# Moving the first attention scores ahead of four running-maximum steps, and adding unit-matrix products at the start of a one-core block kernel

## The chip, the core and the metric

The kernel runs on one core of a Trainium2 chip. The metric is the device time of one execution in microseconds (us); several executions are timed and the median is given. A separate execution was recorded by the hardware profiler; times inside it are counted from the start of its span.

## What is computed

The input is x of 8 sequences, 512 tokens, 128 features (float32). With xn = layernorm(x), the output is x + attention(xn) + ffn(xn). Cut to what matters:

```
q, k: (b, s, 8 heads, 2, 8)      v: (b, s, 8 heads, 16)
scores = einsum('bqhif,bkhif->ibhqk', q, k) * 8 ** -0.5
att    = softmax(scores)[0] - diff_weight * softmax(scores)[1]
o      = einsum('bhqk,bkhe->bqhe', att, v)
attention = (rms_normalized(o) * norm_w) @ Wo.T + bo, times (1 - diff_weight)
gates  = sigmoid(xn @ Wg); the best 2 of 8 experts per token, weights normalized
ffn    = (shared expert + weighted sum of 2 routed experts) / 3
```

Each expert is silu(x @ W1) * (x @ W3) @ W2 with 256 inner features. The matrices are float32 throughout.

## The kernel before, in words

**Tiling.** A sequence b has NT = 4 token tiles of 128. Its 8 heads are worked in four pairs w; a pair has u = 0, 1. In the tensors qst and kst (two of each, taken in turn by the sequences) head 2w+u is one slab of 128 partitions by 512 tokens; the two halves of the partitions (ROWS) are the two halves i of the differential attention.

**Two passes over the scores.** The softmax needs the maximum over keys per query before the exponential. So `maxima(b, w)` (L786) goes through eight steps for a pair (u by t): two matmuls into the PSUM tile mx (L795) and one reduction on VectorE into the tile most (L802). The tile mx has one buffer; for the first pair alone (b = w = 0) every second step uses the buffer of sc instead. After the eighth step the maxima are split into two parts (L808, L809) and `shift(b, w)` (L825) puts them into spare rows of qst, so that the scores come out with the maximum already subtracted. For the first pair this goes by a TensorE transpose (L829, pm), a copy on ScalarE (L831, first_rows) and two DMAs of SP's queue (L820). `scores(b, w, c, u)` (L840) then makes two matmuls for one key tile (L844, sc) and the exponential on ScalarE (L852, pe); `weigh` multiplies by the values (L863, av). `next_maxima(n)` (L1049) takes the next n steps of all maxima in order; with 8 sequences, 4 pairs, 8 steps there are 256.

**Order of the work.** The order of instructions on every engine is the order of the program, written out by hand. It has a start-up part (L1062 to L1188) and a main loop (L1215 to L1251) of 128 steps of two half steps each. A half step makes one `scores` and one step of maxima, which runs ahead by a fixed number of steps. Beside these, `pieces(step)` (L1190) picks other work from a list of jobs with due steps, by estimated cost (ROOM) and free PSUM banks: norms and gates of later sequences, routing, the experts, the shared expert, the folding of results. A job's parts come at "soon" or "late" places of a step. In the first half step the job prepare(1) makes pq (L727), in the third pv (L771) and a transpose px (L236).

**Lead of the maxima.** AHEAD is 11: start-up makes 11 steps of maxima before the loop (eight of pair 0, three of pair 1). The loop adds one more in its first half step (`turns <= 1`, L1241), so that the lead is 12 steps from then on.

**Start-up in the order of TensorE.** Four weight transposes (L1090, pw); four transposes of xn (L236, px); head(0, 0), head(0, 1) (L1118, pd, each followed by a ScalarE step L1120 and a VectorE step L1123 that write the first slabs of qst and kst); maxima step 1; head(1, 0); step 2; head(1, 1); the products pq of the other six heads (L727); steps 3 to 8 with px of sequence 1, pv (L771), gate products (L249) between; then steps 9 to 11. `keep_clock()` (L1148) is a product of the unit matrix with xnT whose result (idle) nobody reads. It stands once before step 4, before step 6 (after the gate products), before step 7 and before step 8, and twice at each of steps 9, 10 and 11 (L1170 to L1173). In the trace one such product shows as two MATMUL records.

**Copies of sequence 0.** prepare(0) splits q and k in an upper and a lower part (L738, L740), and sixteen DMAs (`copy`, L753) spread them into rows of qst and kst. For sequence 0 those of qst are issued from SP's queue and those of kst from ScalarE's queue, four each for upper and lower.

**Other names.** L184 is the VectorE memset of heads 2 to 7 of kst[0] to 1.0. L1095 is a VectorE copy of pw, L213 to L217 are the statistics of the norm. The pool ps_3 holds three PSUM buffers of one bank (tag mm) that the temporary products take in turn; ps_1 holds single ones (av, sc, mx).

Of the kernel before, what the change touches and what calls it, by code (L numbers as in the profile page):

```python
# [11 lines left out]
F32 = mybir.dt.float32  # L12
# [19 lines left out]
def kernel(  # L32
# [52 lines left out]
    nc = tc.nc  # L85
    B, S, E = x.shape
    NT = S // P
    NE, _, FF = We1.shape
# [19 lines left out]
    def small_psum(name):  # L108
        return ps_3.tile([P, S], F32, tag="mm", name=name)
# [26 lines left out]
    ident = const.tile([P, P], F32, name="ident")  # L136
# [41 lines left out]
    kst = []  # L178
# [28 lines left out]
    def norm(b):  # L207

        xt = xn[b]
        stats = p2.tile([P, NT, 6], F32, tag="stats", name=f"stats_{b}")  # L210
        both = p2.tile([P, NT, 2], F32, tag="both", name=f"both_{b}")
        for t in range(NT):
            nc.vector.bn_stats(stats[:, t, :], xt[:, t, :])  # L213
        for t in range(NT):
            nc.vector.bn_aggr(both[:, t, :], stats[:, t, :])
        rstd = p2.tile([P, NT], F32, tag="rstd", name=f"rstd_{b}")
        nc.vector.tensor_scalar(rstd, both[:, :, 1], LN_EPS, None, ALU.add)  # L217
        nc.gpsimd.tensor_tensor(rstd, rstd, minus_half, ALU.pow)
        yield
        for t in range(NT):  # L220

            (nc.gpsimd if b else nc.vector).tensor_scalar(  # L222
                xt[:, t, :], xt[:, t, :], both[:, t, 0:1], rstd[:, t : t + 1], ALU.subtract, ALU.mult
            )
        yield
# [6 lines left out]
    def turn(b):  # L232

        px = small_psum(f"px_{b}")
        for t in range(NT):
            nc.tensor.transpose(px[:, t * P : (t + 1) * P], xn[b][:, t, :], ident)  # L236
        xnT = p3.tile([P, S], F32, tag="xnT", name=f"xnT_{b}")
        return xnT, px
# [306 lines left out]
    turns = 0  # L545
# [169 lines left out]
    def prepare(b):  # L715

        st = state[b]
        if "xnT" not in st:
            yield 0.45, 1
            st["xnT"], px = turn(b)  # L720
            yield "late"
            nc.scalar.copy(st["xnT"], px)
        xnT = st["xnT"]
        yield 1.75, 2
        pqs = [small_psum(f"pq_{b}_{i}") for i in range(2)]
        for i in range(2):
            nc.tensor.matmul(  # L727
                pqs[i],
                w_c[:, i].rearrange("p i f u -> p (i f u)") if b else w_rest[:, i],
                xnT,  # L730
                start=True,
                stop=True,
            )
        parts = []
        for i in range(2):
            yield ("soon", "late")[i]
            upper = p1.tile([P, S], F32R, tag=f"upper{i}", name=f"upper_{b}_{i}")
            nc.scalar.copy(upper, pqs[i])  # L738
            lower = p1.tile([P, S], F32R, tag=f"lower{i}", name=f"lower_{b}_{i}")
            nc.vector.tensor_tensor(lower, pqs[i], upper.bitcast(F32), ALU.subtract)  # L740
            parts.append((upper, lower))
        q, k = qst[b % 2], kst[b % 2]

        def no_shift():
            for half in range(2):
                nc.sync.dma_start(
                    out=q[64 * half + SHIFT : 64 * half + SHIFT + 2]
                    .bitcast(F32)
                    .rearrange("p u s -> p (u s)"),
                    in_=noughts,  # L750
                )

        def copy(part, i, s):  # L753

            row_of = (2 * part + s, part + 2 * s)[i]
            first = 0 if b else 2
            for half in range(2):
                (nc.scalar if b == 0 and i else nc.sync).dma_start(
                    out=(q, k)[i][64 * half + row_of : 64 * half + STACK : 4, first:, :].bitcast(F32),
                    in_=parts[i][part][64 * half : 64 * half + F * (H - first), :].bitcast(F32),  # L760
                )

        if b > 1:
            copies.append(no_shift)
        for part, i in ((0, 0), (0, 1), (1, 0), (1, 1)):
            for s in range(2):
                copies.append(lambda part=part, i=i, s=s: copy(part, i, s))
        yield 0.9, 1
        pv = small_psum(f"pv_{b}")
        for t in range(NT):  # L770
            nc.tensor.matmul(  # L771
                pv[:, t * P : (t + 1) * P],
                xnT[:, t * P : (t + 1) * P],
                w_t[:, 0, :],
                start=True,
                stop=True,
            )
        yield "late"
        nc.scalar.copy(
            vals[b % 2].rearrange("p t h e -> p (t h) e")[:, :, 0:DH],  # L780
            pv.rearrange("p (n e) -> p n e", e=DH),
        )
# [57 lines left out]
    def scores(b, w, c, u):  # L840

        sc = ps_1.tile([P, 2, S], F32, tag="sc", name=f"sc_{b}_{w}_{c}_{u}")
        for i in range(2):
            nc.tensor.matmul(  # L844
                sc[:, i, :],
                kst[b % 2][ROWS[i], 2 * w + u, c * P : (c + 1) * P],
                qst[b % 2][ROWS[i], 2 * w + u, :],
                start=True,
                stop=True,
            )  # L850
        pe = p4.tile([P, 2, S], F32, tag="pe", name=f"pe_{b}_{w}_{c}_{u}")
        nc.scalar.activation(pe, sc, AF.Exp, scale=F**-0.5)  # L852
        return pe
# [111 lines left out]


    STEPS = 4 * NT
    AHEAD = 11
    MIX = 30
    EACH = 4.65  # L970
    ROOM = 2.25
# [49 lines left out]
    def run(part):  # L1021
        for _ in part:
            pass
# [25 lines left out]
    def next_maxima(n):  # L1049
        for _ in range(n):  # L1050
            found = next(tiles, None)
            if found is None:
                return
            b, w, k = found
            if k == 0:
                streams[b, w] = maxima(b, w)
            next(streams[b, w])
            if k == 7:
                run(streams.pop((b, w)))
                shift(b, w)  # L1060

    with tc.manual_schedule():  # L1062
# [3 lines left out]

        norms = {b: norm(b) for b in range(B)}
        next(norms[0])  # L1070
        rows = const.tile([P, 5], F32, name="rows")
# [13 lines left out]
            nc.vector.tensor_scalar(signs[:, i : i + 1], lower, -2.0, 1.0, ALU.mult, ALU.add)  # L1085
        run(norms[0])

        pw = ps_1.tile([P, S], F32, tag="av", name="pw")
        for i in range(4):
            nc.tensor.transpose(pw[:, i * P : (i + 1) * P], w_raw[:, i, :], ident)  # L1090
# [13 lines left out]
        xnT, px = turn(0)  # L1104
# [37 lines left out]
            w = pw[:, i * P : (i + 1) * P]  # L1142
            nc.scalar.copy(w_c[:, i], w.rearrange("p (u i f) -> p i f u", i=2, f=F))
        nc.scalar.copy(w_t.rearrange("p i e -> p (i e)"), pw[:, 2 * P :])

        idle = ps_1.tile([P, S], F32, tag="av", name="idle")

        def keep_clock():  # L1148
            nc.tensor.matmul(idle, ident, xnT, start=True, stop=True)  # L1149

        next_maxima(1)
        state[1]["xnT"], px = turn(1)
        nc.scalar.copy(state[1]["xnT"], px)
        keep_clock()
        next_maxima(1)
        run(first)
# [6 lines left out]
        next_maxima(1)  # L1163
        gates(1, state[1]["xnT"])
        held.append(pgs[0])
        keep_clock()
        next_maxima(1)
        keep_clock()
        next_maxima(1)
        for _ in range(AHEAD - 8):  # L1170
            keep_clock()
            next_maxima(1)
            keep_clock()  # L1173
        sides = const.tile([P, 1], F32, name="sides")
        nc.vector.memset(sides, 1.0)
# [42 lines left out]
        while step < total + 1 or jobs or errands or loads:  # L1218
            for second_half in range(2):
                if step < total:  # L1220
                    b, r = divmod(step, STEPS)
                    w, c = divmod(r, NT)
                    pe = scores(b, w, c, second_half)
                    pes = [pe] if not second_half else pes + [pe]
                if shifted:
                    shifted.popleft()()
                next_maxima(1)
                turns += 1
                if errands:

                    if latest:
                        nc.gpsimd.tensor_copy(mark, latest.pop())  # L1232
                    errands.popleft()()

                if copies and (turns % 3 or not loads):
                    copies.popleft()()
                elif loads:
                    loads.popleft()()
                if not second_half:
                    begun = pieces(step)  # L1240
                    if turns <= 1:  # L1241
                        next_maxima(1)
                    follow(begun, "soon")
                else:
                    follow(begun, "late")
                    if last is not None:
                        weigh(*last)
                    if turns <= 1:
                        next_maxima(1)
                    last = (b, w, c, pes) if step < total else None  # L1250
            step += 1  # L1251
# [48 lines left out]
```

## Time and profile before

| | us |
|---|---|
| three timed executions | 670.26, 674.56, 678.87 |
| median | 674.56 |
| the profiled execution, its own time | 684.2 |
| its span, first to last instruction | 682.3 |
| outside the span | 1.9 |
| first scores (L844) begin | 46.22 |

In the span TensorE is busy for 625.5 us (92%), VectorE for 518.2 (76%), ScalarE for 357.5 (52%), GpSimd for 278.7 (41%). The profiled execution is 9.6 us longer than the median and 5.3 us longer than the longest of the three timed ones. Busy shares are means over stages: in some stretches VectorE is the fuller engine, and the clock that is granted to TensorE is not the same in all of them.

How to read the lines: a group or a timeline entry gives the start, the duration, the engine (PE is TensorE, PEld its weight loads, DVE is VectorE, ACT ScalarE, POOL GpSimd, SPq and ACTq the DMA issue of two queues), the code line, the operation, the tile written and the tiles read, and in brackets the idle time before it with what ended it. Ends of matmuls are modelled, so that a busy TensorE is not necessarily at its peak.

### The profile page before, as it was taken

The numbers are of one execution on the slowest core, as the hardware profiler recorded it, in microseconds if no ns is written. First come the engines' busy times: TensorE is split into PE (matmuls) and PEld (weight loads), VectorE is DVE, ScalarE is ACT, GpSimd is POOL, SyncE is SP. The second block draws the span as 40 slices with busy tenths as digits, with TensorE's granted clock in tenths as the row PEclk, the third lists the DMA queues.
The fourth block names the chain that finished last, engine by engine and source line by source line (L and its number), as shares of the span: only waits on it lengthen the run. The fifth ranks groups of instructions, "written<-read, shape, count | busy, mean of one in ns | idle before, by whom it ended". The sixth has DMA issues, their size and how long they took to land.

```text
span 682.3 us, 10940 instructions
## 1 busy us (share of the span) xinstructions
PE 625.5 (92%) x3781; PEld 329.0 (48%) x3781; DVE 518.2 (76%) x945; ACT 357.5 (52%) x435; POOL 278.7 (41%) x455
## 2 busy tenths in 40 slices
PE   4988998789998999999999999999999999999874
PEld 1424543245543554556555554455555655555222
DVE  7658658997778787767777777867778687778983
ACT  2214543453445655566555655656466655555552
POOL 7516600048704144544544444553445425523101
PEclk9978867796989999999999999999999999999997
DMA  5222332021500233435462234435353234401360
GB/s 168 75 89 69 117 105 95 26 73 59 155 26 22 72 97 122 153 115 161 127 181 86 85 121 136 148 122 155 119 188 92 100 98 149 121 18 30 131 220 33
DMA packets 41665, 72.64 MB, mean 106 GB/s; under 512 B 10581, under 2 KB 15862, under 8 KB 41586
## 3 DMA queue, kind: packets, MB, share of 16 engines
q1 hardware_dynamic: 35978, 61.05, 28.2%
q0 software_dynamic: 4608, 9.45, 4.8%
q10 hardware_dynamic: 1024, 1.44, 0.7%
q8 instruction: 30, 0.49, 0.3%
q14 instruction: 25, 0.20, 0.1%
HBM read 46.19 MB, written 12.60 MB: 86 GB/s over the span
## 4 chain that ended last, share of the span: by engine, by line
PE 70%; DVE 21%; issue 5%; ACT 3%; POOL 0%; DVEq 0%; ACTq 0%; POOLq 0%
PE sc L844 13%; PE av L863 13%; PE mx L795 10%; DVE most L802 10%; PE ph L632 8%; PE py L645 5%; PE ps L885 3%; ACT pe L852 3%; PE ph L959 2%; PE pi L435 2%; PE po L903 2%; PE pq L727 2%; PE idle L1149 2%; PE pg L249 1%; PE pz L942 1%
## 5 line engine op out<-in xcount | busy, mean ns | idle before, releaser
L802 DVE TENSOR_REDUCE most<-mx 128x2 f32<-128x1024 f32 x256 | 312.8, 1222 | 107.4 <-PE mx L795 107.0
L852 ACT ACTIVATE pe<-sc 128x1024 f32<-128x1024 f32 x256 | 262.4, 1025 | 241.4 <-PE sc L844 239.5
L844 PE MATMUL sc<-qst,kst 64*128 64x512 f32 x512 | 131.6, 511 | 12.5 <-ACT pe L852 12.2
L863 PE MATMUL av<-pe,vals 128*32 128x512 f32 x1024 | 142.7, 630 | 0.0
L795 PE MATMUL mx<-kst,qst 64*128 64x512 f32 x512 | 123.1, 472 | 16.4 <-DVE most L802 14.5
L844 PEld LDWEIGHTS sc<-qst,kst 64*128 64x128 f32 x512 | 49.0, 188 | 157.4 <-ACT pe L852 115.7
L569 POOL DMA_INDIRECT xq<-tokens,tokens_at x72 | 71.1, 987 | 37.2 <-issue 27.0
L657 POOL DMA_INDIRECT results<-y,results_at x72 | 70.8, 984 | 36.5 <-issue 31.4
L795 PEld LDWEIGHTS mx<-kst,qst 64*128 64x128 f32 x512 | 51.4, 193 | 62.2 <-DVE most L802 50.9
L1232 POOL COPY mark<-most 1x2 f32<-1x2 f32 x144 | 25.4, 176 | 136.8 <-DVE most L802 134.2
L632 PE MATMUL ph<-xT,w 128*128 128x128 f32 x576 | 74.8, 281 | 1.0 <-DVE r L946 0.9
L632 PEld LDWEIGHTS ph<-xT,w 128*128 128x128 f32 x576 | 67.6, 191 | 9.3 <-issue 6.6
L914 POOL TENSOR_TENSOR o<-on 128x128 f32<-128x128 f32 x32 | 14.8, 462 | 137.8 <-DVE on L910 137.7
L863 PEld LDWEIGHTS av<-pe,vals 128*32 128x32 f32 x1024 | 20.6, 109 | 43.0 <-issue 42.8
L645 PE MATMUL py<-w,h 128*128 128x128 f32 x288 | 38.4, 283 | 2.8 <-DVE h L609 2.8
L645 PEld LDWEIGHTS py<-w,h 128*128 128x128 f32 x288 | 33.9, 191 | 8.0 <-issue 4.1
L606 DVE SCALAR_TENSOR_TENSOR th<-th,ph 128x512 f32<-128x512 f32 x36 | 24.6, 685 | 14.1 <-ACT th L605 14.1
L885 PE MATMUL ps<-xnT,s 128*128 128x512 f32 x64 | 32.1, 620 | 0.6 <-DVE on L910 0.6
L605 ACT ACTIVATE th<-ph 128x512 f32<-128x512 f32 x36 | 21.5, 597 | 15.6 <-PE ph L632 13.7
L873 ACT ACTIVATE ov<-av,sides 128x512 f32<-128x512 f32 x32 | 22.2, 694 | 6.8 <-PE av L863 6.5
L609 DVE TENSOR_TENSOR h<-th,ph 128x512 f32<-128x512 f32 x36 | 24.1, 669 | 0.0
L222 POOL TENSOR_SCALAR xn<-xn,both,rstd 128x128 f32<-128x128 f32 x28 | 22.0, 797 | 0.7
(161 smaller groups left out, 600.3 us busy)
## 6 DMA issues: line engine op xcount, KB each, us to landing
w<-experts SPq DMA_DIRECT2D x72, 384.0 KB
ym<-results SPq DMA_DIRECT2D x16, 256.0 KB
qst<-upper SPq DMA_DIRECT2D x28, 128.0 KB
kst<-upper SPq DMA_DIRECT2D x28, 128.0 KB
qst<-lower SPq DMA_DIRECT2D x28, 128.0 KB
kst<-lower SPq DMA_DIRECT2D x28, 128.0 KB
experts<-in_L_ffn_We_dram SPq DMA_DIRECT2D x24, 128.0 KB
r<-in_L_attn_x_dram SPq DMA_DIRECT2D x8, 256.0 KB
```

Of the source, the lines that this page charges most:

```text
L569: nc.gpsimd.indirect_dma_start(out=xq[:, n, :], out_offset=None, in_=tokens[:, :], in_offset=bass.IndirectOffsetOnAxis(ap=tokens_at[:, j : ...
L606: nc.vector.scalar_tensor_tensor(th, th, 1.0, ph, ALU.add, ALU.mult)
L632: nc.tensor.matmul(ph[:, ns], ws[n][:, f : f + P], xT[:, ns], start=True, stop=True)
L645: nc.tensor.matmul(py[:, ns], hs[c][:, ns], ws[n][:, f : f + E], start=(c == 0), stop=(c == NF - 1))
L657: nc.gpsimd.indirect_dma_start(out=results_of[j], out_offset=bass.IndirectOffsetOnAxis(ap=results_at[:, j : j + 1], axis=0), in_=y[:, n, : ...
L795: nc.tensor.matmul(sc[:, i, :], q[ROWS[i], 2 * w + u, t * P : (t + 1) * P], k[ROWS[i], 2 * w + u, :], start=True, stop=True,)
L802: nc.vector.tensor_reduce(most[:, t, u, :], sc, AX.X, ALU.max, negate=True)
L844: nc.tensor.matmul(sc[:, i, :], kst[b % 2][ROWS[i], 2 * w + u, c * P : (c + 1) * P], qst[b % 2][ROWS[i], 2 * w + u, :], start=True, stop=True,
L852: nc.scalar.activation(pe, sc, AF.Exp, scale=F**-0.5)
L863: nc.tensor.matmul(st["av"][32 * g : 32 * g + 32, :], vals[b % 2][:, c, 2 * w + u, :], pes[u][:, i, :], start=(c == 0), stop=(c == NT - 1),)
L885: nc.tensor.matmul(ph, w[:, c * P : (c + 1) * P], st["xnT"], start=True, stop=True)
L1232: nc.gpsimd.tensor_copy(mark, latest.pop())
```

## The change

Four edits.

1. The constant AHEAD becomes 12, and the condition of the extra steps of maxima in the loop becomes `turns <= AHEAD - 8`, that is 4. Start-up makes only the eight steps of the first pair; the first scores follow, and each of the first four half steps makes one step of maxima more than the later ones. After four half steps the lead is 12, as before after the first.
2. The unit-matrix product is defined at the outset, on a temporary PSUM buffer and with a slab of kst[0] (memset to 1.0 by L184) as its moving operand. Four of them are put ahead of the weight transposes pw. Later the names are bound to the tile av and to xnT, as before.
3. The number of products between the steps changes: two instead of one before step 4, two instead of one before step 7 and before step 8, four behind step 8 and nothing of the six at steps 9 to 11.
4. The four DMAs that spread the upper part of k of sequence 0 go from ScalarE's queue to SP's; those of the lower part stay on ScalarE's.

```diff
@@ copy(), L758
-                (nc.scalar if b == 0 and i else nc.sync).dma_start(
+                (nc.scalar if b == 0 and i and part else nc.sync).dma_start(
@@ L968
-    AHEAD = 11
+    AHEAD = 12
@@ before norms, L1069
+        idle = small_psum("idle")
+        some = kst[0][:, 2, :].bitcast(F32)
+
+        def keep_clock():
+            nc.tensor.matmul(idle, ident, some, start=True, stop=True)
+
@@ before pw, L1088
+        for _ in range(4):
+            keep_clock()
         pw = ps_1.tile([P, S], F32, tag="av", name="pw")
@@ L1146
         idle = ps_1.tile([P, S], F32, tag="av", name="idle")
-
-        def keep_clock():
-            nc.tensor.matmul(idle, ident, xnT, start=True, stop=True)
-
+        some = xnT
         next_maxima(1)
         state[1]["xnT"], px = turn(1)
         nc.scalar.copy(state[1]["xnT"], px)
         keep_clock()
+        keep_clock()
         next_maxima(1)
@@ L1166
-        keep_clock()
-        next_maxima(1)
-        keep_clock()
-        next_maxima(1)
-        for _ in range(AHEAD - 8):
+        for _ in range(2):
+            keep_clock()
             keep_clock()
             next_maxima(1)
+        for _ in range(4):
             keep_clock()
@@ L1241 and L1248
-                    if turns <= 1:
+                    if turns <= AHEAD - 8:
                         next_maxima(1)
```

More of the change, by code (lines that the diff above doesn't have):

```diff
@@ L1247 @@
                         weigh(*last)
-                    if turns <= 1:
+                    if turns <= AHEAD - 8:
                         next_maxima(1)
```

## The prediction

> **What bounds the kernel now.** I read the page first, for which engine is full and at which clock.
>
> ```profile
> PE 625.5 (92%) x3781; PEld 329.0 (48%) x3781; DVE 518.2 (76%) x945; ACT 357.5 (52%) x435; POOL 278.7 (41%) x455
> PEclk9978867796989999999999999999999999999997
> ```
>
> TensorE is 92% busy, and from the thirteenth slice on its clock is full. In slices 3 to 12 (34 to 205 us) it often is not. So I asked for the busy times by stage, with the loop's entry as one stage. The columns are PE, PEld, DVE, ACT, POOL busy, then the granted clock.
>
> ```profile
> 35.90:46.20 10.30, 10.27 (x19) 3.33 (x19) 3.37 (x3) 0.26 (x1) 0.00 (x0) 0.68 0.42 131
> 46.20:57.70 11.50, 9.32 (x43) 4.83 (x42) 9.04 (x22) 5.25 (x7) 6.99 (x15) 0.85 0.00 0
> 57.70:80.00 22.30, 19.38 (x132) 10.11 (x132) 18.64 (x59) 13.38 (x17) 18.69 (x23) 1.00 0.36 110
> 80.00:97.00 17.00, 17.00 (x70) 8.43 (x63) 7.25 (x7) 6.63 (x9) 0.00 (x0) 0.50 0.46 148
> 200.00:660.00 460.00, 444.06 (x2904) 242.19 (x2903) 357.33 (x592) 270.63 (x330) 191.93 (x324) 1.00 0.37 115
> ```
>
> The reader is to see three regimes. Up to 80 us neither engine is full for long: TensorE and VectorE wait for each other through the one mx buffer. From 80 to 97 TensorE is full because it runs at half clock. From 200 on it is full at full clock (97%), and nothing of the change is there. So the change is worth what it moves the point at which the fifth half step begins, plus what it does to the clock. The chain in order of time shows what sets that point.
>
> ```profile
> 33.96 1.24 DVE most L802
> ...
> 36.33 1.71 PE idle L1149 x2
> 38.03 0.72 PE mx L795 x2
> 38.76 3.71 PE idle L1149 x4
> 42.47 0.43 PE mx L795
> 42.90 1.91 PE idle L1149 x4
> 44.81 0.42 PE mx L795 x2
> 45.23 1.05 PE idle L1149 x2
> 46.29 0.42 PE sc L844 x2
> ```
>
> Of the 10.3 us from the eighth maximum's end to the first scores, 8.4 are unit products: 1.7 to 1.9 each at first, 0.95 to 1.05 after 42.4. The timeline gives the other durations.
>
> ```profile
> 10.21 3.75 PE L1118 MATMUL pd<-xnT,four_rest 128*128 128x512 f32 x4 [0.72 <-DVE both L215]
> 24.59 1.21 DVE L802 TENSOR_REDUCE most<-mx 128x2 f32<-128x1024 f32 x1
> 27.43 3.97 ACTq L758 DMA_DIRECT2D kst<-upper  x4
> 36.64 1.37 SPq L820 DMA_DIRECT2D qst<-first_rows  x2
> 50.73 0.50 PE L795 MATMUL mx<-kst,qst 64*128 64x512 f32 x2 [1.09 <-DVE most L802]
> 52.55 0.71 PE L795 MATMUL mx<-kst,qst 64*128 64x512 f32 x2 [1.09 <-DVE most L802]
> ```
>
> The two pd products of 10.21 take 1.9 each, the later idle ones 1.0: until about 22 us TensorE runs at half speed, whatever the clock record (1.00 there) says. And where VectorE limits, one step of maxima costs 52.55 - 50.73 = 1.82 us, which is the reduction of 1.22 and the 0.6 until the next mx stands.
>
> **The change part by part.**
>
> **1. Four products ahead of pw.** They can begin when the memset of kst ends (4.06), so at 4.15. At half clock four take 4 x 1.9 = 7.6, ending at 11.8. When the clock comes decides. In the rows by 4 us it went full within 36 to 44 at 42.4, which is 6.5 us after dense work began at 35.9; that row puts it at 10.7. The Trainium skill (TensorE: Matmul & The Clock Gate, What's actually happening) says that a free-running window of about 3.4 us must be busy; that puts it anywhere between 7.6 and 11, and the steps of this trace's clock, at 35.6, 42.4, 52.6, 56.1, 80.0 and 97.0, are multiples of 3.41 apart, whose grid puts it at 8.3 in this phase. I take 8.3: 4.15 us cold hold 2.2 products, the other 1.8 take 1.9, end 10.2 (by the row alone 11.3). pw and px behind them take 1.3 at full clock, so px ends at 11.5 instead of 9.5. **Cost 2.0.** Then two pd at 1.05 instead of 1.9 give back 1.7, so the first mx comes at 15.9 instead of 15.6. Up to the third reduction stand two more pd and two pq, of which all but the last pq were slow; that gives about 2.6, so that reduction begins at 22.3 instead of 24.6. **Net of the head: -2.3**, between +3 (cold throughout: px ends 3.6 us later, at 13.1, and only waits of TensorE give some of it back) and -4 (clock at 7.6, and all products behind it at full speed). The same section speaks against the idea: it puts the whole warm-up below 1% of a usual span, here 6.8 us, as a ceiling, and a third of that is what I find.
>
> What these products are moved past: VectorE's copies L1095 wait for pw until about 10.9 instead of 8.9, and behind them in its queue are the norms of sequences 1 and 2 (2.8 us) and the first L1123. These end at 14.2, about when ScalarE's first L1120 is ready (14.1), so it is covered, barely. The PSUM buffer taken from the ring of three is released long before its next use: nothing.
>
> **2. Three more products before steps 4, 7 and 8.** From 24 to 33 the chain is TensorE's own (idle, mx, pv, pg in turn), so they aren't hidden: 3 x 1.05 = **+3.1**. The eighth reduction ends at 35.2 - 2.3 + 3.1 = 36.0.
>
> **3. The kst upper copies to SP.** SP then issues 12 where it issued 8, at 0.75 each: from about 21 (the cast of q is earlier too) to 30. Behind them on SP are the first rows, which aren't there before 37. The four of qst lower now stand behind four more issues, 3 us later; their first reader is step 9, in the new order beyond 41. ScalarE loses 4 us of issue ahead of the copy L831, which had its queue clear at 35.5 for a pm at 36.3. **Zero**, covered by 4 us or more; without the cover (a start-up faster by 4) it would be a gain of up to the same 4.
>
> **4. First scores behind the eighth step.** Splitting takes 0.7, pm 0.4, so products begin at about 37.1: four take 4.2 warm or 7.6 cold. First rows: L831 0.3, two issues 1.4, landing about 1.6 after the last issue by the turned rows (issue at 59.04, reader at 61.27), 40.6 in all: hidden behind the products. TensorE is idle for 1.7 us before pm, as before, where the clock fell; scores start at 41.5 or 44.9. I take 43.0 against 46.2: **-3.2**, which contains parts 1 and 2.
>
> **5. Three maxima in half steps 2 to 4.** Below: TensorE time only, 3 x 0.5 = 1.5, if pv, px and the cold stretch at 52.6 hide the reductions. Above: 3 x 1.82 = 5.5, and 1.5 more if that stretch is long. I laid the order out: reductions 9 to 16 with the two L740 and the statistics between them, each mx waiting for the reduction before. From first scores to the end of reduction 16 it takes 17.4 where the trace has 11.9. VectorE is the limit nearly throughout, so I take the upper row, **+5.5**. What is late next: reduction 17, step 5's mx, and so everything behind it, since both queues are in order.
>
> **Sum:** -3.2 + 5.5 = +2.3; ends -3 (41.5 and +1.5) and +6 (44.9 and +7). Own time 684.2 would become 686.5. The execution shown lies 9.6 above the median of the three runs; the difference goes onto the median: 674.6 + 2 = **676.5**. What had looked like eleven microseconds of start-up was a place where VectorE did three reductions; they go to a place where VectorE is the limit.
>
> **Rule against row on the clock.** The same page (Why this matters for your kernels) asks for no idle gap above about 3 us. In the loop's entry no gap is that long, before or after, so by the rule the clock would stay full, and part 5 would be some 1.5 less: 675. The trace differs: it fell at 52.6 behind gaps of 1.1, and at 80.0 with TensorE 85% busy (3.38 of 4 us) in the slice before. The trace decides, so I keep the fall.
>
> **The rivals.**
>
> - **The entry stays cold (slower).** Between 80 and 97 the mixture of sc, mx, pg, px and av ran at half clock, fully busy, and didn't get the clock back until the dense ps. There half steps take 3.2 (81.11 to 94.0, four), against 2.17 (62.86 to 78.02, seven). With maxima doubled TensorE waits more for VectorE in half steps 2 and 3, and if pv and px don't bring the clock back as they did at 56.1, it stays half to 97: 22.3 / 2.17 = 10 half steps by 1.03, and four at the entry by 1, is +15, and +2 of above: 691. It decides where no busy window falls between 52 and 58. For: the fall at 52.6. Against: pv and px stand there again. Chance 0.18.
> - **The clock holds (faster).** Filler up to the first scores, no single-buffer wait with TensorE idle. Cold time from 36 to 200 is about 54 us; at about a third lost each, with no such time at all, 18 us go: 684.2 - 18 = 666, and with 41.5 as the start 662. Over 2% (below 661) takes all of it. For: the three runs spread by 8.6, so some of this varies. Against: the stretches after 97 come from work that isn't touched. Chance 0.08 for over 2%.
> - **The start isn't earlier.** Cold products at outset and again behind step 8 put the first scores at 45 to 46; then the extra maxima cost fully: 680. Chance 0.2, within 2%.
> - **The extra maxima are hidden.** 671 to 673, chance 0.22, within 2%.
>
> **How the numbers follow.** My forecast (673 to 680) has 0.32; with the last two, within 2% has 0.74. Two per cent, 13.5 us, is about what a measurement of this kernel can tell from no change. Slower 0.18, faster 0.08. The range of eight in ten leaves out the ends of the clock's two cases: 664 to 691. The likeliest case's own range with its neighbours is 668 to 683.
>
> **What would show it.** Right: pd at about 1.0 from 12 us on; first scores at 41 to 45; the last of 16 reductions ending at 59 to 62 instead of 58.1; two mx per half step 1.8 apart; SP's twelve issues done by 31. Wrong: the sixteenth reduction before 56 (extra maxima hidden), first scores beyond 46, or a granted clock of 0.5 from 52 through 80, or none below 1 up to 200.

## The result, and the profile after

Over 20 executions each, the changed kernel takes 676.92 us in the median (674.36 to 684.67), the kernel before 673.66 (668.13 to 682.27). The ratio is 1.0074, 95% interval 1.0047 to 1.0101: slower by 0.7%, 5.0 us of 673.7 (3.2 to 6.8). Within two per cent that counts as no change, but the interval does not hold 1. The ratio leaves out the unusually long executions, which the two medians, 3.3 us apart, still hold; the profiled execution of the kernel before (684.2) is one of them, which matters below.

First the page of the kernel after, its busy times and its clock by fortieths of the span.

```profile
PE 614.5 (91%) x3791; PEld 323.3 (48%) x3791; DVE 518.7 (77%) x945; ACT 357.4 (53%) x435; POOL 278.0 (41%) x455
PEclk9886999899999999999999999999999999999898
```

TensorE has less busy time than before (614.5 against 625.5) and a span shorter by 6.8 us (675.5 against 682.3). Read alone, the two profiles say that the change made the kernel faster; twenty timed executions of each say the opposite. The stages show where this comes from (columns as before: PE, PEld, DVE, ACT, POOL, then the clock).

```profile
35.90:46.20 10.30, 8.58 (x21) 3.38 (x21) 3.64 (x12) 1.86 (x3) 3.24 (x10) 0.83 0.33 103
46.20:57.70 11.50, 6.04 (x24) 3.80 (x24) 8.21 (x16) 3.26 (x4) 4.16 (x5) 0.72 0.12 37
57.70:80.00 22.30, 19.67 (x116) 8.90 (x116) 17.39 (x52) 10.84 (x15) 14.73 (x18) 0.84 0.29 91
80.00:97.00 17.00, 16.44 (x108) 8.12 (x104) 11.98 (x18) 10.72 (x15) 3.54 (x5) 1.00 0.47 148
200.00:660.00 460.00, 442.74 (x2896) 240.81 (x2894) 360.42 (x607) 271.65 (x331) 191.87 (x325) 1.00 0.38 118
```

In this execution 80 to 97 runs at full clock (1.00 against 0.50), and the loop's entry, 46 to 80, at a lower one than before (0.72 and 0.84 against 0.85 and 1.00). From 200 on almost nothing differs. At the end of reduction 24 (the 24th step of maxima) the changed kernel is 4.5 us behind (80.55 against 76.06); at reduction 32 it is 2.6 ahead (97.84 against 100.39), because of the half clock that the profiled execution before had from 80 to 97. The other 4.2 of the 6.8 us come after that, and up to 200 the execution before again ran more at half clock than the one after (0.87 against 0.97):

```profile
97.00:200.00 103.00, 89.20 (x490) 44.04 (x489) 87.53 (x166) 44.99 (x49) 36.24 (x55) 0.87 0.22 72
97.00:200.00 103.00, 85.30 (x518) 41.83 (x511) 90.22 (x173) 46.97 (x52) 36.11 (x55) 0.97 0.23 73
```

A kernel that differs from the one before only in a queue (below) had full clock from 80 to 97 and ended reduction 32 at 90.82; against it the changed kernel is 7.0 us behind there, and 7.0 at the end of the span (675.5 against 668.5).

How usual is the profiled execution before? Each timed execution comes with its mean granted clock. In one series of 60 executions of the kernel before, the four below 0.958 took 681.6 to 685.1 us, and the twelve at 0.980 or more took 670.2 to 673.7. The profiled one has 0.954. So executions of one and the same kernel differ by up to 15 us, and the longest are those with the most half clock. At an equal mean clock the loss of the changed kernel remains: its four executions at 0.972 took 676.3 to 677.5, while the 28 executions of the kernel before at 0.972, in all series, have a median of 672.4.

The chain, in order of time, from the last reduction of start-up to the first scores:

```profile
35.63 1.24 DVE most L802
...
37.60 0.39 PE pm L829
37.99 4.95 PE idle L1074 x8
42.94 0.43 PE sc L844 x2
```

The scores begin at 42.9 behind four products, and no maxima stand between: three steps of them (9 to 11) have moved behind the scores; the twelfth stood behind them in the kernel before too. The timeline of the entry, TensorE and VectorE:

```profile
47.27 0.50 PE L795 MATMUL mx<-kst,qst 64*128 64x512 f32 x2 [1.09 <-DVE most L802]
48.95 0.86 DVE L213 BATCH_NORM_STATS2 stats<-xn 128x6 f32<-128x128 f32 x4
49.09 0.50 PE L795 MATMUL mx<-kst,qst 64*128 64x512 f32 x2 [1.32 <-DVE most L802]
...
50.24 0.69 DVE L740 TENSOR_TENSOR lower<-pq,upper 128x512 fp32r<-128x512 f32 x1
50.85 1.22 DVE L802 TENSOR_REDUCE most<-mx 128x2 f32<-128x1024 f32 x1
...
52.12 0.80 PE L795 MATMUL mx<-kst,qst 64*128 64x512 f32 x2 [2.29 <-DVE most L802]
52.84 2.08 PE L771 MATMUL pv<-w_t,xnT 128*128 128x128 f32 x8
...
57.82 0.80 PE L795 MATMUL mx<-kst,qst 64*128 64x512 f32 x2 [0.90 <-DVE most L802]
58.65 1.23 DVE L802 TENSOR_REDUCE most<-mx 128x2 f32<-128x1024 f32 x1 [0.89 <-PE mx L795]
```

The brackets show what bounds it: each mx waits for the reduction before it, up to 2.29 us. VectorE was at work up to the end of that longest wait: the statistics of a norm (L213) and the split of a product (L740) stand in its queue between two reductions. Then, at half clock, mx takes 0.80 instead of 0.50 and pv 2.08 instead of the 1.16 that it takes at full clock, and now a reduction waits 0.89 for TensorE.

### The profile page after: what moved, and what is told of

Its sections match the earlier page's. It is cut to its first block, busy times and chain, and to the rows that moved or that the text cites. A ratio compares the mean times of both kernels' runs of the same rounds, so it can differ in the third digit from the quotient of the medians.

```text
span 675.5 us, 10962 instructions
## 1 busy us (share of the span) xinstructions
PE 614.5 (91%) x3791; PEld 323.3 (48%) x3791; DVE 518.7 (77%) x945; ACT 357.4 (53%) x435; POOL 278.0 (41%) x455
## 4 chain that ended last, share of the span: by engine, by line
PE 69%; DVE 22%; issue 5%; ACT 4%; POOL 0%; DVEq 0%; ACTq 0%; POOLq 0%
PE sc L844 12%; PE av L863 12%; DVE most L802 11%; PE mx L795 10%; PE ph L632 9%; PE py L645 5%; PE ps L885 3%; ACT pe L852 3%; PE idle L1074 3%; PE po L903 2%; PE pq L727 2%; PE pi L435 2%; PE ph L959 2%; DVE what L456 1%; PE pz L942 1%
## 5 line engine op out<-in xcount | busy, mean ns | idle before, releaser
L802 DVE TENSOR_REDUCE most<-mx 128x2 f32<-128x1024 f32 x256 | 312.9, 1222 | 102.1 <-PE mx L795 101.4
L863 PE MATMUL av<-pe,vals 128*32 128x512 f32 x1024 | 140.2, 619 | 0.0
L844 PE MATMUL sc<-qst,kst 64*128 64x512 f32 x512 | 129.2, 501 | 11.2 <-ACT pe L852 10.9
L844 PEld LDWEIGHTS sc<-qst,kst 64*128 64x128 f32 x512 | 48.4, 186 | 151.1 <-ACT pe L852 116.6
L606 DVE SCALAR_TENSOR_TENSOR th<-th,ph 128x512 f32<-128x512 f32 x36 | 24.7, 685 | 14.1 <-ACT th L605 14.1
L605 ACT ACTIVATE th<-ph 128x512 f32<-128x512 f32 x36 | 21.5, 597 | 15.4 <-PE ph L632 13.8
```

The lines of the kernel that those rows point to most:

```text
L606: nc.vector.scalar_tensor_tensor(th, th, 1.0, ph, ALU.add, ALU.mult)
L802: nc.vector.tensor_reduce(most[:, t, u, :], sc, AX.X, ALU.max, negate=True)
L844: nc.tensor.matmul(sc[:, i, :], kst[b % 2][ROWS[i], 2 * w + u, c * P : (c + 1) * P], qst[b % 2][ROWS[i], 2 * w + u, :], start=True, stop=True,
L863: nc.tensor.matmul(st["av"][32 * g : 32 * g + 32, :], vals[b % 2][:, c, 2 * w + u, :], pes[u][:, i, :], start=(c == 0), stop=(c == NT - 1),)
```

## The experiments

Each kernel was timed in five rounds against the kernel before on the same chip. I cut start-up and entry of every profiled execution into four pieces by the reductions L802 and the first L844: the end of reduction 3; from there to the end of reduction 8; from there to the first scores; from there to the end of reduction 16 (all in us). Each row shows one execution, the ratio many.

| kernel | red. 3 ends | to red. 8 | to scores | to red. 16 | ratio (95% interval) |
|---|---|---|---|---|---|
| before | 25.8 | 9.4 | 11.0 | 11.9 | 1 |
| after | 24.9 | 12.0 | 6.0 | 19.6 | 1.0074 (1.0047 to 1.0101) |
| outset only | 22.8 | 9.4 | 11.1 | 11.9 | 0.9975 (0.9948 to 1.0002) |
| order only | 26.3 | 9.4 | 6.1 | 19.7 | 1.0053 (1.0029 to 1.0076) |
| after, spread | 22.9 | 12.0 | 6.1 | 18.8 | 1.0004 (0.9980 to 1.0027) |
| before, no products at 9 to 11 | 24.7 | 11.0 | 6.0 | 15.4 | 0.9996 (0.9967 to 1.0025) |
| outset and queue | 24.9 | 9.4 | 8.6 | 11.2 | 0.9951 (0.9931 to 0.9972) |
| three products only | 24.4 | 12.0 | 8.0 | 11.2 | 1.0023 (0.9991 to 1.0055) |
| after, products in the entry | 23.0 | 12.0 | 6.1 | 17.2 | 1.0028 (1.0005 to 1.0051) |
| spread, lean | 24.5 | 9.4 | 4.4 | 17.4 | 0.9960 (0.9938 to 0.9982) |
| queue only | 24.2 | 9.4 | 8.6 | 11.2 | 1.0003 (0.9977 to 1.0030) |
| spread, lean, products | 22.9 | 9.4 | 6.0 | 17.4 | 0.9978 (0.9952 to 1.0004) |
| outset, queue, one product each | 24.6 | 9.4 | 7.3 | 12.3 | 0.9961 (0.9939 to 0.9982) |
| after, lean | 22.8 | 9.4 | 6.0 | 19.6 | 1.0011 (0.9990 to 1.0033) |

**The four parts alone.** The outset's products on the kernel before (their definition moves up with them, which the cut leaves out):

```diff
+        for _ in range(4):
+            keep_clock()
         pw = ps_1.tile([P, S], F32, tag="av", name="pw")
```

> The kernel before with the four unit products ahead of the weight transposes and nothing else changed. My theory (they gain about 1 us at the third reduction, 23.7 in the changed kernel against 24.6, and touch nothing later): first scores about 45.3, ratio to before 0.998 to 1.000. Rival (the outset delays more than the early clock gives back, and is part of the loss): first scores at 47 or later, ratio 1.002 or more.

0.9975: it gains a little, or nothing at the interval's end; scores began at 43.3, earlier than expected. The four products themselves, first in the changed kernel, then in "after, lean":

```profile
4.20 6.65 PE L1074 MATMUL idle<-kst,ident 128*128 128x512 f32 x8 [4.20 <-DVE stats L213]
4.20 5.97 PE L1073 MATMUL idle<-kst,ident 128*128 128x512 f32 x8 [4.20 <-DVE stats L213]
```

What this difference means is said with the prediction's first term below. The order alone:

```diff
-    AHEAD = 11
+    AHEAD = 12
...
         keep_clock()
         next_maxima(1)
-        for _ in range(AHEAD - 8):
-            keep_clock()
-            next_maxima(1)
+        for _ in range(4):
             keep_clock()
...
-                    if turns <= 1:
+                    if turns <= AHEAD - 8:
```

> The kernel before with the first scores behind the eighth step, four unit products behind that step and none at steps 9 to 11, and three more maxima in half steps 2 to 4; without the outset's products, with one product each before steps 4, 7 and 8 as before, and the copies on their old queue. My theory (the loss is the three extra maxima at a place where VectorE is the limit): from first scores to the end of reduction 16 it takes 17 to 20 us against 11.9, and although scores begin at 41 to 44 the ratio is 1.003 to 1.008. Rival (the loss is the three added products in start-up): scores begin 2 to 3 us earlier than in the changed kernel and the ratio is 0.998 to 1.002.

1.0053, and 19.7 us from scores to reduction 16. The rival's mark, scores two to three us before those of the changed kernel, didn't come (41.7 against 42.9). The order is the greater part of the loss. The three added products:

```diff
+        keep_clock()
         keep_clock()
         next_maxima(1)
         run(first)
...
-        keep_clock()
-        next_maxima(1)
-        keep_clock()
-        next_maxima(1)
+        for _ in range(2):
+            keep_clock()
+            keep_clock()
+            next_maxima(1)
```

> The kernel before with three unit products more, two in place of one before steps 4, 7 and 8, nothing else changed. My theory (they stand on TensorE's own chain, 1.05 us each): reduction 8 ends at 37.5 to 38.5 instead of 35.2, everything behind it is 3 us later, ratio 1.003 to 1.005; with the outset (0.9975) and the order (1.0053) the three parts then make the whole of 1.0074. Rival (they hold the clock up to the first scores and pay for themselves): reduction 8 at 38 but first scores at 47 or earlier, ratio 0.998 to 1.001.

In the trace they cost 2.6 us (12.0 in every kernel that has them, 9.4 in all others but one); the ratio of 1.0023 is inconclusive by itself. Taking them out of the changed kernel was the second try:

```diff
         keep_clock()
-        keep_clock()
         next_maxima(1)
         run(first)
...
-        for _ in range(2):
-            keep_clock()
-            keep_clock()
-            next_maxima(1)
+        keep_clock()
+        next_maxima(1)
+        keep_clock()
+        next_maxima(1)
```

> The changed kernel without its three added products before steps 4, 7 and 8; all else as changed. In the kernel before they gave 1.0023 with an interval that holds zero; between the two spread kernels 0.0044. If they stand on the path (3.1 us): ratio 1.002 to 1.004, against 1.0074 with them, and reduction 8 ends about 10 us behind reduction 3 instead of 12. If they are hidden: 1.006 or more.

1.0011 against 1.0074: on the path. The difference, 4.2 us, is more than 2.6, but the two intervals together leave it that room; 1.0011 also lies below the 1.002 that was expected. This kernel and "outset and queue" differ in the order alone, so the order's cost is shown a second time: 1.0011 against 0.9951, 4.0 us. The queue alone:

```diff
-                (nc.scalar if b == 0 and i else nc.sync).dma_start(
+                (nc.scalar if b == 0 and i and part else nc.sync).dma_start(
```

> The kernel before with only the four copies of kst upper moved to SP's queue. My theory: nothing waits for either queue at this place, ratio 0.998 to 1.002. Rival (the queue is a part of the result, since the outset gave 0.9975 without it and 0.9951 with it): 0.996 to 0.998.

1.0003, nothing. On SP's queue the edit brings a wait, which nothing behind it felt. In the changed kernel, the four issues and the wait between them (total, times, longest):

```profile
25.34 6.07 SPq L758 DMA_DIRECT2D kst<-upper  x4
SPq L758 <- DMA kst<-lower: 3.3, 1, 3.3
```

The four parts alone (-0.0025, +0.0053, +0.0023, +0.0003) add up to +0.0054; that the whole is +0.0074 lies within the intervals. The queue kernel's trace shows the kernel before with its clock at full where the profiled execution had half. Its stages from reduction 8 to the scores, to reduction 16, and 80 to 97:

```profile
33.60:42.10 8.50, 7.68 (x19) 2.71 (x19) 3.94 (x7) 0.26 (x1) 0.00 (x0) 1.00 0.40 122
42.10:53.30 11.20, 8.62 (x45) 3.93 (x44) 9.38 (x22) 5.88 (x8) 6.67 (x15) 1.00 0.12 35
80.00:97.00 17.00, 16.07 (x86) 6.21 (x84) 13.18 (x21) 9.73 (x13) 0.46 (x1) 1.00 0.55 184
```

With six products and three steps of maxima the scores begin at 42.1, earlier than in the changed kernel. Of the 4.1 us to the 46.2 of the profile before, 1.6 stand ahead of reduction 3; the rest is in the 11.0 us from reduction 8, of which 2.4 were half clock and no work. That the queue held the clock isn't likely: "three products only", with the old queues, has it at 1.00 in this stretch too (8.0), while "outset only", also with the old queues, has half clock (11.1): with the old queues both occur.

**Is it VectorE or the clock?** Three unit products were added in the loop of the changed kernel, where TensorE waits for reductions:

```diff
                     if turns <= AHEAD - 8:
                         next_maxima(1)
+                        if turns == 3:
+                            keep_clock()
                     follow(begun, "soon")
...
                     if turns <= AHEAD - 8:
+                        if turns == 2:
+                            keep_clock()
                         next_maxima(1)
+                        if turns == 2:
+                            keep_clock()
```

> The changed kernel with three unit products more inside the loop: two in half step 2 around its extra step of maxima, one behind that of half step 3, in gaps in which TensorE waits for reductions. If the clock at 0.5 from 51 to 62 is a cause of its own: it stays at 1.00 there, reduction 16 ends 17 to 18 us after the first scores begin instead of 19.6, and the ratio falls from 1.0074 to 1.003 to 1.005. If VectorE alone sets the entry: the clock is held but reduction 16 still takes 19 us or more, ratio 1.006 to 1.010.

Windows of the changed kernel from 51.2 and of this one from 49.4, each up to its reduction 16:

```profile
51.20:62.50 11.30, 8.56 (x32) 4.30 (x32) 6.99 (x14) 2.81 (x4) 4.52 (x7) 0.55 0.00 1
```

```profile
49.40:58.20 8.80, 6.00 (x34) 2.86 (x34) 6.85 (x14) 3.91 (x5) 4.35 (x6) 1.00 0.00 0
```

```profile
45.87 1.13 PE L1074 MATMUL idle<-xnT,ident 128*128 128x512 f32 x2
47.26 0.49 PE L795 MATMUL mx<-kst,qst 64*128 64x512 f32 x2 [0.27 <-DVE most L802]
47.68 1.13 PE L1074 MATMUL idle<-xnT,ident 128*128 128x512 f32 x2
...
50.28 0.49 PE L795 MATMUL mx<-kst,qst 64*128 64x512 f32 x2 [1.04 <-DVE most L802]
```

Two of the three products fill waits (0.27 is left of 1.32, 1.04 of 2.29), the clock holds, and the entry takes 17.2 instead of 19.6: work that nobody reads makes the kernel faster, 1.0028 against 1.0074 (the intervals just touch). So both are causes. At full clock the extra maxima cost 17.2 - 11.2 = 6.0 up to reduction 16, the half clock 2.4 more. Counted on to reduction 24, where later falls of the clock come in, it is 35.1 from the scores here, 37.7 in the changed kernel and 29.8 in the profile before: 5.3 for the maxima and about 2.5 for the half clock.

**Where the extra maxima stand.** They were moved to half steps 1, 3, 5 and 7, with the number unchanged:

```diff
-                    if turns <= AHEAD - 8:
+                    if turns < 8 and turns % 2:
```

> The changed kernel with its four extra steps of maxima in half steps 1, 3, 5 and 7 in place of 1, 2, 3 and 4. My theory (single mx buffer and VectorE are the limit at the entry): spreading leaves the number of reductions the same, and VectorE is nearly full to half step 8 too, so of the 5 us only 1 to 2 come back: ratio 1.003 to 1.006, reduction 24 ends at 78 to 80. Rival (it is the doubling in one half step that lets TensorE idle and its clock fall): the clock stays at 1.00 between 51 and 62 and the ratio is 0.998 to 1.001.

1.0004: the gain is larger than I expected, yet the rival's mark is absent, for the clock was half from about 47 to 56 and again later. The trace doesn't explain the gain: from scores to reduction 24 it takes 37.3 us, the changed kernel 37.7. Of the 2.5 us between the two spans (673.0 and 675.5), 2.0 stand ahead of reduction 3, where nothing differs between the two kernels. So the gain stays open. Next, the same without the three added products:

```diff
         keep_clock()
-        keep_clock()
         next_maxima(1)
         run(first)
...
-        for _ in range(2):
-            keep_clock()
-            keep_clock()
-            next_maxima(1)
+        keep_clock()
+        next_maxima(1)
+        keep_clock()
+        next_maxima(1)
```

> The changed kernel with the four extra steps of maxima in half steps 1, 3, 5 and 7 and without the three added products before steps 4, 7 and 8; the outset's products and the queue edit stay. My theory (the parts add up): 1.0004 of the spread kernel less 0.0045 for the products, 0.994 to 0.998, first scores at 38 to 41. Rival (with fewer products the clock falls at the first scores and takes it back): first scores at 41 or later or half clock from 36 to 60, ratio 0.999 to 1.003.

0.9960, the sum that was expected, and the earliest scores but one, at 38.3. Then it ran for 24 us at half clock:

```profile
51.00:74.60 23.60, 20.46 (x84) 9.52 (x80) 15.74 (x50) 7.68 (x9) 12.45 (x15) 0.51 0.24 75
```

Three products were to hold it:

```diff
+                if 1 <= turns <= 3:
+                    keep_clock()
                 next_maxima(1)
                 turns += 1
```

> The kernel with the lean start-up and the extra maxima in half steps 1, 3, 5 and 7 (0.996), with one unit product more in each of half steps 2, 3 and 4 between the scores and the maxima, in gaps of 1.1 us. If the half clock from 50 to 75 us is what that kernel still loses (about 8 us by the trace): the clock holds past 55, reduction 24 ends at 70 to 73 instead of 78.7, ratio 0.986 to 0.993. If it only falls later, in the next such stretch: ratio 0.994 to 0.998, with a stretch at 0.5 elsewhere before 100.

0.9978, no better than without. In the profiled execution the clock held to about 53 and was at 0.55 from 52 to 75: the fall had only moved, as the second case said. But this execution took 681.6 against a median of 672.6, so the trace shows what can happen and not what mostly does.

**Fewer products, maxima ahead of the scores.** The kernel before without the six products at steps 9 to 11:

```diff
         for _ in range(AHEAD - 8):
-            keep_clock()
             next_maxima(1)
-            keep_clock()
```

> The kernel before without the six unit products at steps 9 to 11, so that these three steps stand directly behind the eighth and the first scores behind them; nothing else changed. My theory (the time from step 8 to the first scores was unit products, not maxima): three steps of 1.8 us end at about 42, scores at 42 to 43 with the lead of the maxima complete, reduction 16 at 54 to 56 instead of 58.1, ratio 0.994 to 0.998. Rival (the products hold the clock that the loop's entry needs): the clock is at 0.5 from about 36 on through the first half steps, reduction 16 ends at 58 or later, and the ratio is 1.000 to 1.010.

```profile
38.98 0.80 PE L795 MATMUL mx<-kst,qst 64*128 64x512 f32 x2 [1.32 <-DVE most L802]
41.10 0.79 PE L795 MATMUL mx<-kst,qst 64*128 64x512 f32 x2 [1.32 <-DVE most L802]
...
43.94 3.53 PE L727 MATMUL pq<-xnT,w_c 128*128 128x512 f32 x4
```

Three steps of maxima fit in the 6.0 us that the changed kernel spends on four products, so the scores begin as early with three steps more done. But pq takes 3.53 instead of 1.98, at a clock of 0.50 from 36.8 to 47.1, the entry 15.4 instead of 11.2, and the ratio is 0.9996: what was won ahead of the scores was lost behind them. It also tells the moved maxima from the missing products: without products at steps 9 to 11, but with these steps ahead of the scores, there is no loss; with the steps behind them ("order only", four products) there is one of 0.53%. With the outset and the queue edit, and the old order:

```diff
+        for _ in range(4):
+            keep_clock()
         pw = ps_1.tile([P, S], F32, tag="av", name="pw")
...
-                (nc.scalar if b == 0 and i else nc.sync).dma_start(
+                (nc.scalar if b == 0 and i and part else nc.sync).dma_start(
```

> The kernel before with the outset's four products and the four copies of kst upper on SP's queue, nothing else of the change. The outset alone gave 0.9975. My theory (the queue edit costs and gains nothing: ScalarE's issues end 1.4 us before the copy of the first rows even then): 0.996 to 0.999, first scores at 43 to 45.5. Rival (twelve issues on SP delay the first rows or step 9): first scores 2 us later, ratio 1.000 or more.

0.9951, the lowest ratio of all, and faster than the kernel before and the changed one. Since the queue alone is 1.0003, its share over the outset's 0.9975 isn't shown; the intervals overlap. And with one product in place of two at each of steps 9 to 11:

```diff
         for _ in range(AHEAD - 8):
             keep_clock()
             next_maxima(1)
-            keep_clock()
```

> The kernel with the outset's products and the queue edit (0.9951), the order as before, and one unit product in place of two at each of steps 9 to 11, ahead of the maxima; the wait for the reduction before is 1.1 us, so one product fits it. My theory: first scores at 40 to 41.5 instead of 42.9 with the lead complete and the clock held, ratio 0.990 to 0.994. Rival (three products fewer, the clock falls before the loop, as without any): half clock from about 36 on, reduction 16 at 54 or later, ratio 0.996 to 1.000.

0.9961, not better, and not the 0.990 to 0.994 expected: 1.3 us were won before the scores (7.3 against 8.6), 1.1 given back behind them (12.3 against 11.2). The clock was at half from 37.0 to 40.4, as the rival had it, but full in the entry, so the 1.1 stay unexplained.

## Why the prediction was right, and which terms of it were off

The forecast was 676.5 and no change beyond two per cent; the median is 676.9. The verdict was right for the reason given: small terms of opposite sign. That the two times lie 0.4 apart is luck: the base taken, 674.6, was 0.9 above the 673.7 of twenty executions, and the change added, 2, was below the 3.3 between the medians and the 5.0 of the ratio. By the forecast's steps:

- **The outset.** Forecast -2.3 at the third reduction. The nine kernels with the products end it at 23.7 in the mean, the five without at 25.1: -1.4. It has two values, 22.8 to 23.0 and 24.5 to 24.9. In the four kernels that end it later the clock falls at 16.3 to 17.0 us for 3.4 us, and the pd after it are slow again; in the five that end it earlier it stays at 1.00 to beyond 30. The forecast left that fall out. It also took the time of full clock, 8.3, from the grid of one execution, and the next has it at another place: the four products begin at 4.2 in all nine kernels and take 5.96 to 6.18 us in the five, 6.29 to 6.65 in the four. With 1.9 us per product at half and 0.95 at full clock, full clock comes, as an estimate, at 8.5 for the shortest and at 9.9 for the longest. Why the clock falls again in the four isn't shown. The ceiling of 6.8, an estimate that the forecast drew from the Trainium skill (TensorE: Matmul & The Clock Gate, What's actually happening) held: 1.4 is a fifth of it.
- **The three products.** Forecast +3.1, measured 2.6 (9.4 to 12.0), on the path as said.
- **The queue.** Forecast zero, measured 1.0003. But the cover was thinner than worked out: the four issues of kst upper take 0.67 each, and between the second and the third SP waits 3.3 us, which the trace puts down to a DMA of kst lower. That wait was not in the sum. SP was done at 34.3, not 30, still 4.0 ahead of the first rows at 38.3.
- **First scores.** Forecast 43.0, measured 42.9, in part by luck: reduction 8 ended 0.9 later than forecast (36.9 against 36.0), and from there it took 6.0 instead of 7.0. What was wrong is what they were set against. The forecast's 10.3 us begin at 35.9; from the end of reduction 8 it is 11.0, of which 2.4 was half clock in the one execution shown. With the clock full the old order takes 8.6 and starts its scores at 42.1. So there were 2.6 to win here, and the three products took 2.6: next to nothing was left of the -3.2.
- **The extra maxima.** Forecast 17.4 from scores to reduction 16, hence +5.5; with the clock full it is 17.2, against 11.2, hence +6.0. The mechanism, mx and reduction in turn through one buffer, is in the brackets. "VectorE is the limit nearly throughout" says too much: in the 17.2 us VectorE is busy for 13.3, and it is the turn-taking that fills the rest. No run gave mx a second buffer, so what that would bring is not shown. The half clock that the range allowed for came: 19.6, hence +2.4 more, and reduction 16 ended at 62.5, just beyond the 59 to 62 named as a sign.

With the measured terms up to reduction 16: -1.4 + 2.6, then 6.0 against 8.6 to the scores (-2.6), then 6.0 + 2.4, make +7.0 against a kernel before with full clock. Against one whose clock falls as in the profile (11.0 and 11.9) it is -1.4 + 2.6 - 5.0 + 7.7 = +3.9. The measured +5.0 lies between, which proves little: the traces themselves are 9.2 and 4.4 apart at reduction 16, 7.0 and 4.5 at reduction 24, since the clock falls at other places behind the entry. The forecast's +2.3 has the right sign and is half of the 5.0; the gain before the scores was sized too large (the fourth point), and the half clock in the entry was left out of the likeliest value (the fifth).

Of the rivals, the cold entry came in part: half clock from 51, as foreseen, but it was back at 61.4, behind pv, px and av, and not at 97 (it fell once more, from 64.8 to 68.2). That the long stretch exists is shown by the lean spread kernel (51 to 75). The holding clock didn't come, and the outset's products don't reach that far: with them or without, the entry is the same (19.6 and 19.7). "The start isn't earlier" is true against a kernel before at full clock. The rule of the same page (Why this matters for your kernels), to leave no idle gap above about 3 us, would have kept it full here; the gap in which it fell was 2.29, the one before it 1.32.

## What to carry to other kernels

Before a stall is removed, look for what the other engine did in it: here three reductions ran under the unit products, and moved behind the scores they cost 5 to 6 us at a place where one buffer makes matmul and reduction take turns. Size a stall from more than one execution, since one profile can hold a fall of the clock that the next doesn't have. Filler that holds the clock can pay where TensorE waits anyway (the entry: 1.0028 against 1.0074, though in the lean spread kernel it brought nothing, 0.9978 against 0.9960), and costs most of its length where TensorE is the chain (2.6 of 3.1 us before steps 4, 7 and 8).

## What was not expected of the hardware

- Unread work shortened the kernel: three products of 1.1 us each, two of them in waits of 1.32 and 2.29 us, took 2.4 us off the entry.
- Half clock can last with TensorE busy throughout: 17.00 of 17 us in the profile before, 20.46 of 23.6 in the lean spread kernel. The place changes from one profiled execution or variant to the next (80 to 97, 51 to 75), and with it which of two profiles looks shorter. The executions of the kernel before at a mean clock of 0.980 or more and those below 0.958 lie about 8 to 15 us apart.
- When the copies of one tile were issued from two queues, there was a wait: SP stood for 3.3 us between the second and the third issue of kst upper (3.1 in the queue-only kernel), put down to a DMA of kst lower, which ScalarE's queue issues. Nothing needed SP then; why it waits wasn't tried.
